# Relative-position tables through DRAM, splits and additions placed elsewhere in an eight-image attention kernel

## The chip, the cores and the metric

The kernel runs on one core of a Trainium2 chip. The core has five engines with a queue each: TensorE (PE, matrix products; its weight loads are listed as PEld), VectorE (DVE), ScalarE (ACT), GpSimd (POOL) and SyncE (SP, which here only issues transfers). An engine works through its queue in order. Products land in PSUM; everything else lies in SBUF or in DRAM. The metric is the device time of one execution in microseconds, as the median of the runs.

## What is computed

Eight images of 32 x 32 positions and 384 channels (1024 tokens each) go through two layers.

```
# layer 0, per image; 6 heads of 64
q, k, v = split(groupnorm(x) @ qkv_w + qkv_b)
s  = (q * 64**-0.5) @ k.T
s += rel_h[:, :, :, :, None] + rel_w[:, :, :, None, :]
#    rel_h[y, x, k] = q[y, x] . rel_pos_h[y - k + 31]
#    rel_w[y, x, k] = q[y, x] . rel_pos_w[x - k + 31]
x  = x + softmax(s) @ v @ proj_w + proj_b
# layer 1
x  = x + causal_attention(layernorm(x))       # one head of 384
x  = x + ffn(layernorm(x))                    # images 0 to 4 only
```

The FFN has sign weights, and after each of its two products it scales by the largest absolute value of the image and clips. So its last step can begin only when the whole image's second product is there.

## The kernel before, in words

One image follows another (`run`, L836). For each there are four stages: `layer0` (L421) with projections, positions and values, then `attend0_fast` (L499), `attention1` (L649), and for images 0 to 4 `ffn` (L766). The path named `g` is entered only if a check of the sums at the end asks for it; in the profile it isn't run.

Products in plain fp32 appear as two records each in the profile. To get nearly fp32 results from the cheaper form fp32r, the kernel splits a value into a high part (rounded to fp32r) and a low part (the remainder) and puts both on different partitions of one tile. For q and k this is `hi_lo` (L428): ACT writes the high part of 64 rows (L429), DVE the low part (L430), from PSUM. Heads go in pairs: `q[par]` and `k[par]` hold, for parity `par`, the high part in one half of the partitions and the low part in the other. `ks` is k with the halves exchanged; POOL copies it (L442, L443). A score tile of 128 keys x 1024 queries is then the sum of three fp32r products (L508): k with q, ks with q, and `unit` with `r`.

`r` carries the relative positions: 32 rows of rel_h and 32 of rel_w for each head, high and low parts. `unit` (L175) spreads them over the 32 x 32 keys. In the kernel before, `positions(g)` (L445) makes them for four image rows and four image columns at a time, for all three pairs at once: 16 fp32 products with a window of 32 table columns as weights and 96 queries (L454), then four casts on ACT (L464) and four subtractions on DVE (L465) of 32 x 384 from PSUM into `r`. Eight groups make an image.

The order in the code is q of the three pairs, k of pair 0, and then eight times a position group and a value product (L470, L385), with k of pairs 1 and 2 between them (`queries_keys`, L434). In `attend0_fast` each pair of heads goes through eight chunks of keys: two score tiles, an exp each on ACT (L512), running sums on DVE (L521), products with v on PE (L526), two chunks behind. At the second chunk of pair 0, `residual` loads x (L105) and POOL adds the bias (L491).

`ffn` ends with a reduction over partitions on POOL (L747), eight clamps on POOL (L833) and eight additions on DVE (L834); then SP stores the image (L856).

The queues are not written out by hand: the framework places each engine's instructions when the kernel is built, by their order in the code and by when their operands are expected, and allots the buffers of a pool as they come free. So products of the next image already run inside the FFN (L375 beside L823), though they come later in the code. The pools that matter are `image` (11 tiles of three rows of 1024), `page` (11 tiles of 128 x 1024), and in PSUM `ps_s` (2 score tiles, also used by the projections) and `ps_o` (4 tiles of 512).

Of the kernel before, what the change touches and what calls it, by code (L numbers as in the profile page):

```python
# [9 lines left out]
F32 = mybir.dt.float32  # L10
# [64 lines left out]
def conv_attn_hybrid(  # L75
# [38 lines left out]
    rel = tile_of("rel", [P, 2, 2 * H - 1])  # L114
    qscale = HD**-0.5

    def load_weights():

        nc.scalar.dma_start(out=bqk, in_=qkv_b[0 : 2 * C].rearrange("(m p) -> p m", p=P))
        for half in range(2):  # L120
            nc.scalar.dma_start(out=rel[half * HD : (half + 1) * HD, 0, :], in_=rel_hT)
            nc.scalar.dma_start(out=rel[half * HD : (half + 1) * HD, 1, :], in_=rel_wT)
# [12 lines left out]
        nc.scalar.mul(rel, rel, 1.0 / qscale)  # L135

# [13 lines left out]
    ones = const.tile([P, P], F32, name="ones")  # L150
# [24 lines left out]
    def make_unit():  # L175

        for i in range(4):
            r = slice(32 * i, 32 * (i + 1))
            nc.gpsimd.tensor_copy(
                unit[r].rearrange("i (h w) -> i h w", h=H), ident[r, r].unsqueeze(2 - i % 2).to_broadcast([32, H, W])  # L180
            )
# [6 lines left out]
    def judge(pools):  # L188

        bad = const.tile([P, 2, N_SEEN], F32, name="bad")  # L190
# [89 lines left out]
    def stages(pools):  # L280
# [140 lines left out]
        def layer0(b, xT):  # L421
# [12 lines left out]
            def queries_keys(m):  # L434
                p = m % NPAIR
                ps = project_T(wqkv_sb, ts(m, P), xT, f"qk_{b}_{m}")
                for par in range(2):
# [3 lines left out]
                    if m >= NPAIR:  # L441
                        nc.gpsimd.tensor_copy(ks[par][hi, p, :], dst[lo].bitcast(F32))  # L442
                        nc.gpsimd.tensor_copy(ks[par][lo, p, :], dst[hi].bitcast(F32))  # L443

            def positions(g):  # L445

                ps = pools.o_tile(f"rel_{b}_{g}")[:, :384].rearrange("p (i n) -> p i n", i=4)
                for i in range(4):
                    at = 4 * g + i
                    win = slice(H - 1 - at, 2 * H - 1 - at)  # L450
                    for par in range(2):
                        qv = q[par].bitcast(F32).rearrange("d p (h w) -> d p h w", h=H)
                        for d in range(2):
                            nc.tensor.matmul(  # L454
                                ps[ts(2 * par + d, 32), i, :], rel[:, d, win], qv[:, :, :, at] if d else qv[:, :, at, :],
                                start=True, stop=True,
                            )
                for d in range(2):
                    for par in range(2):
                        hi, lo = 2 * par + d, 2 * (1 - par) + d  # L460
                        dst = r[par].rearrange("k p (h w) -> k p h w", h=H)
# [443 lines left out]
```

## Time and profile before

| | |
|---|---|
| runs | 2661.9, 2664.29 and 2665.3 us; median 2664.29 |
| profiled execution | 2669.85 us, of which 2667.5 us are the span of the profile |
| granted TensorE clock, mean | 0.993 |
| moved by transfers | 82.00 MB, 31 GB/s over the span |
| image 6, first projection to the first score with all parts | 2104.3 to 2167.6 us |
| image 1, the same, behind an FFN | 404.8 to 462.0 us; part of its projections ran earlier, inside the FFN |

In a line of groups, the fields are the line of code, engine, operation, output and input tiles, shapes and count, then busy us and mean ns of one, then the idle time of the engine just before them and what ended it. In the timeline they are start, duration, engine, line and shape, and in brackets the idle time before. The ends of products are modelled, and neighbours overlap: how far apart two of them start says more than a mean.

### The profile page before, as it was taken

To read this page: it belongs to the slowest core of one execution; us is meant where nothing else is said; L and a number is where in the kernel's file an instruction comes from. 1 tells how busy PE (TensorE), PEld (TensorE's weight loads), DVE (VectorE), ACT (ScalarE), POOL (GpSimd) and SP (SyncE) were. 2 spreads that over 40 slices of the span, in tenths; PEclk is the share of its full clock that TensorE was granted. 3 is DMA by queue.
4 is the path that set the end of the run, shared out by engine and by line. 5 is a ranking of instruction groups with operands and counts; after the bars stand their busy time and mean duration, and the time that the engine had idled before them with its cause. 6 is when DMAs were issued, how large, how long until landed. Compare 5 with 4: busy or idle time off the path is not lost.

```text
span 2667.5 us, 28335 instructions
## 1 busy us (share of the span) xinstructions
PE 2574.1 (96%) x11394; PEld 1540.6 (58%) x11394; DVE 1500.6 (56%) x2373; ACT 1058.2 (40%) x1480; POOL 215.5 (8%) x202
## 2 busy tenths in 40 slices
PE   7989999999999999999999999999999999999998
PEld 4645585555765556755457555576555555455554
DVE  4885466663466644666545656347665356525652
ACT  3431274431555413654127443155541254115421
POOL 2010004000030000030000400003100020002000
PEclk9999999999999999999999999999999999999999
DMA  2501101010010001010110101011000100010000
GB/s 93 202 36 59 36 1 48 1 59 3 33 48 1 29 31 36 1 48 1 60 36 1 48 1 59 1 36 48 1 24 0 48 1 1 24 48 1 1 1 25
DMA packets 34572, 82.00 MB, mean 31 GB/s; under 512 B 5120, under 2 KB 27520, under 8 KB 32896
## 3 DMA queue, kind: packets, MB, share of 16 engines
q1 hardware_dynamic: 28496, 56.43, 6.0%
q0 software_dynamic: 2880, 23.59, 2.6%
q8 instruction: 92, 1.51, 0.2%
q10 hardware_dynamic: 3056, 0.08, 0.1%
q14 instruction: 48, 0.39, 0.0%
HBM read 62.79 MB, written 17.30 MB: 30 GB/s over the span
## 4 chain that ended last, share of the span: by engine, by line
PE 88%; DVE 6%; ACT 3%; issue 1%; POOL 1%; DMA 0%; ACTq 0%; DVEq 0%
PE f_s L508 20%; PE f_av L526 12%; PE f_v L385 8%; PE f_qk L375 8%; PE f_s L680 7%; PE f_av L694 7%; PE f_y L784 6%; PE f_y L823 5%; PE f_q L659 5%; PE f_pj L385 4%; PE f_rel L454 3%; PE f_pt L287 1%; POOL f_y L833 1%; DVE f_r L465 1%; ACT f_h L809 1%
## 5 line engine op out<-in xcount | busy, mean ns | idle before, releaser
L512 ACT ACTIVATE f_pr<-f_s 128x1024 f32<-128x1024 f32 x384 | 393.6, 1026 | 445.5 <-PE f_s L508 431.2
L521 DVE TENSOR_TENSOR f_sum<-f_sum,f_pr 128x1024 f32<-128x1024 f32 x288 | 355.1, 1245 | 228.7 <-ACT f_pr L512 226.7
L526 PE MATMUL f_av<-f_pr,f_v 128*64 128x512 f32 x1536 | 351.8, 598 | 0.0
L375 PE MATMUL f_qk<-f_gnT,wqkv_sb 128*128 128x512 f32 x576 | 265.8, 608 | 5.8 <-DVE f_q L430 4.6
L508 PE MATMUL f_s<-f_q,f_k 128*128 128x512 f32 x768 | 257.8, 415 | 13.4 <-ACT f_pr L512 13.3
L508 PE MATMUL f_s<-f_r,unit 128*128 128x512 f32 x768 | 242.5, 397 | 2.5 <-DVE f_r L465 2.5
L508 PE MATMUL f_s<-f_q,f_ks 128*128 128x512 f32 x768 | 242.1, 396 | 0.0
L526 PEld LDWEIGHTS f_av<-f_pr,f_v 128*64 128x64 f32 x1536 | 101.9, 136 | 199.8 <-issue 192.0
L680 PE MATMUL f_s<-f_q,f_lnT 128*128 128x512 f32 (+3 forms) x576 | 200.1, 491 | 0.0
L694 PE MATMUL f_av<-f_v,f_pr 128*128 128x385 f32 x576 | 194.5, 486 | 0.0
L508 PEld LDWEIGHTS f_s<-f_q,f_k 128*128 128x128 f32 x768 | 125.2, 189 | 119.2 <-issue 48.7
L375 PEld LDWEIGHTS f_qk<-f_gnT,wqkv_sb 128*128 128x128 f32 x576 | 107.4, 193 | 129.2 <-issue 120.6
L465 DVE TENSOR_TENSOR f_r<-f_rel,f_r 32x384 fp32r<-32x384 f32 x256 | 139.7, 553 | 53.3 <-ACT f_r L464 47.2
L508 PEld LDWEIGHTS f_s<-f_r,unit 128*128 128x128 f32 x768 | 143.8, 189 | 40.3 <-DVE f_r L465 6.9
L508 PEld LDWEIGHTS f_s<-f_q,f_ks 128*128 128x128 f32 x768 | 145.2, 189 | 34.9
L694 PEld LDWEIGHTS f_av<-f_v,f_pr 128*128 128x128 f32 x576 | 108.6, 190 | 78.6 <-issue 11.5
L680 PEld LDWEIGHTS f_s<-f_q,f_lnT 128*128 128x128 f32 x576 | 100.7, 190 | 71.5 <-issue 47.4
L464 ACT CAST f_r<-f_rel 32x384 fp32r<-32x384 f32 x256 | 118.8, 469 | 50.8 <-PE f_rel L454 25.7
L385 PE MATMUL f_v<-wqkv_sb,f_gnT 128*128 128x384 f32 x384 | 137.9, 495 | 0.0
L385 PE MATMUL f_pj<-wproj_sb,f_oT 128*128 128x384 f32 x384 | 128.1, 490 | 9.6 <-DVE f_oT L574 9.6
L659 PE MATMUL f_q<-f_lnT,wqk 128*128 128x512 f32 x288 | 129.3, 603 | 0.0
L788 ACT ACTIVATE f_h<-f_y,b_sb 128x256 f32<-128x256 f32 x240 | 100.6, 471 | 67.1 <-PE f_y L784 66.2
(156 smaller groups left out, 3239.3 us busy)
## 6 DMA issues: line engine op xcount, KB each, us to landing
f_gnT<-in_xT SPq DMA_DIRECT2D x24, 512.0 KB, 4.4
f_x<-in_x SPq DMA_DIRECT2D x32, 384.0 KB, 4.3
out_y<-f_x SPq DMA_DIRECT2D x32, 384.0 KB, 2.5
f_w1a<-w1s POOLq DMA_DIRECT2D x5, 1536.0 KB, 6.8
f_w2a<-w2s POOLq DMA_DIRECT2D x5, 1536.0 KB, 7.0
f_wrest<-w1s POOLq DMA_DIRECT2D x5, 768.0 KB, 4.6
f_wrest<-w2s POOLq DMA_DIRECT2D x5, 768.0 KB, 8.6
wqkv_sb<-in_qkv_w SPq DMA_DIRECT2D x3, 576.0 KB, 6.8
```

The source lines that it names most:

```text
L375: nc.tensor.matmul(ps[:, half, :], w[:, k, cols], xT[:, k, ts(half, 512)], start=(k == 0), stop=(k == NC - 1),)
L385: nc.tensor.matmul(ps[:, :C], xT[:, k, ts(j, P)], w[:, k, cols], start=(k == 0), stop=(k == NC - 1))
L465: nc.vector.tensor_tensor(dst[ts(lo, 32)], src, dst[ts(hi, 32)].bitcast(F32), ALU.subtract)
L508: nc.tensor.matmul(sc[:, half, :], keys[:, ts(c, P)], queries[:, ts(half, 512)], start=(i == 0), stop=(i == 2))
L512: nc.scalar.activation(pr, sc.rearrange("p a n -> p (a n)"), AF.Exp)
L521: nc.vector.tensor_tensor(sums[par], prev, prs[par], ALU.add)
L526: nc.tensor.matmul(avs[half][ts(par, HD), :], v[:, c, ts(h, HD)], prs[par][:, ts(half, 512)], start=(c == 0), stop=(c == NJ - 1),)
L659: nc.tensor.matmul(ps, wqk[:, k, ts(m, P)], xT[:, half, k, :], start=(k == 0), stop=(k == NC - 1))
L680: nc.tensor.matmul(sc[:, half, lo:], xT[:, c // 4, k, ts(c % 4, P)], q[:, half, k, lo:], start=(k == 0), stop=(k == NC - 1),)
L694: nc.tensor.matmul(av[:, : C + 1], prs[c][:, ts(j - c, P)], v[:, c, :], start=(c == 0), stop=(c == j))
L784: nc.tensor.matmul(ps, w1k[i // 2][:, ts(m, P)], xs[i % 2][:, half, i // 2, :], start=(i == 0), stop=(i == 2 * NC - 1))
L823: nc.tensor.matmul(ps[:, :C], h, w, start=(i == 0), stop=(i == len(products) - 1))
```

## The change

- **Positions by pair.** `positions(p)` takes one pair at a time. The whole table of both directions (63 columns each, padded to 64, in high and low part: `rel_split`, made once at the start) is multiplied with the pair's q: for each parity and each half of the queries two fp32r products of 128 x 512, summed in PSUM. ACT copies the 64 rows of rel_h from PSUM, DVE those of rel_w with the two image axes exchanged, into a page of 128 x 1024. SP stores both pages to DRAM (`far`) and reads them back with a stride of one row and 32 elements (`near`): so each of the 32 rows gets its window of the table. That is four transfers of 32 x 32 runs of 32 numbers.
- **Splits by pair.** `split(p, near)` writes `r` from `near`: four casts on ACT and four subtractions on DVE of 32 x 1024, from SBUF. Pair 0's stands before the values, pair 1's behind them, and pair 2's inside the attention, behind the first value products of pair 0 (in image 0 before the attention).
- **Order.** All six projections come first, with the position products of pair p behind the next projection, and then the values.
- **Swapped keys.** `ks` is made by four transfers on SP for each pair, instead of POOL.
- **Last additions.** In images 0 to 4 the eight additions and the store of the result are held back until the next image has issued its q, pair 0's keys and its position products. The clamps on POOL stay where they were.
- `unit` is turned round to fit the table's order; the tables are given unreversed. A few constant tiles are smaller or in pages.

```diff
-            def positions(g):
...
+            def positions(p):
+
+                fars = []
+                for par in range(2):
+                    page = pools.page(f"far_{b}_{p}_{par}")
+                    by_col = page.rearrange("i (w h) -> i w h", h=H)
+                    for half in range(2):
+                        ps = pools.o_tile(f"rel_{b}_{p}_{par}_{half}")
+                        for i in range(2):
                             nc.tensor.matmul(
-                                ps[ts(2 * par + d, 32), i, :], rel[:, d, win], qv[:, :, :, at] if d else qv[:, :, at, :],
-                                start=True, stop=True,
+                                ps, rel_split[:, i].rearrange("d a n -> d (a n)"), q[par][:, p, ts(half, 512)],
+                                start=(i == 0), stop=(i == 1),
                             )
+                        nc.scalar.copy(page[:HD, ts(half, 512)], ps[:HD])
+                        nc.vector.tensor_copy(
+                            by_col[HD:, :, ts(half, H // 2)], ps[HD:].rearrange("i (h w) -> i w h", w=W)
+                        )
+                    far = store.tile([P, T], F32, tag=f"far_{p}_{par}", bufs=2, name=f"{pools.path}_far_{b}_{p}_{par}")
+                    nc.sync.dma_start(out=far, in_=page)
+                    fars.append(far)
+                near = pools.page(f"near_{b}_{p}")
+                for par in range(2):
+                    start = fars[par][0:1, 0:1]
+                    for d in range(2):
+                        src = bass.AP(start.tensor, start.offset + d * HD * T, [[T, 32], [T + 32, 32], [1, 32]])
+                        nc.sync.dma_start(
+                            out=near[ts(2 * par + d, 32)].rearrange("m (n o) -> m n o", n=32), in_=src
+                        )
+                return near
+
+            def split(p, near):
                 for d in range(2):
                     for par in range(2):
                         hi, lo = 2 * par + d, 2 * (1 - par) + d
-                        dst = r[par].rearrange("k p (h w) -> k p h w", h=H)
-                        dst = dst[:, :, :, ts(g, 4)] if d else dst[:, :, ts(g, 4), :]
-                        src = ps[ts(hi, 32)].rearrange("k i (p t) -> k p t i" if d else "k i (p t) -> k p i t", p=NPAIR)
+                        dst = r[par][:, p, :].rearrange("k (h w) -> k h w", h=H)
+                        src = near[ts(hi, 32)].rearrange("k (w h) -> k h w" if d else "k (h w) -> k h w", h=H)
                         nc.scalar.copy(dst[ts(hi, 32)], src)
                         nc.vector.tensor_tensor(dst[ts(lo, 32)], src, dst[ts(hi, 32)].bitcast(F32), ALU.subtract)
...
                     if m >= NPAIR:
-                        nc.gpsimd.tensor_copy(ks[par][hi, p, :], dst[lo].bitcast(F32))
-                        nc.gpsimd.tensor_copy(ks[par][lo, p, :], dst[hi].bitcast(F32))
+                        nc.sync.dma_start(out=ks[par][hi, p, :].bitcast(F32), in_=dst[lo].bitcast(F32))
+                        nc.sync.dma_start(out=ks[par][lo, p, :].bitcast(F32), in_=dst[hi].bitcast(F32))
...
-            for m in range(NPAIR):
+            near = []
+            for m in range(2 * NPAIR):
                 queries_keys(m)
-
-            queries_keys(NPAIR)
-            for g in range(NJ):
-                positions(g)
-                if g in (1, 3):
-                    queries_keys(NPAIR + 1 + g // 2)
-                values(g)
+                if 0 < m <= NPAIR:
+                    near.append(positions(m - 1))
+                if m == NPAIR and unfinished:
+                    unfinished.pop()()
+            split(0, near[0])
+            for j in range(NJ):
+                values(j)
+            split(1, near[1])
+
+            later = [lambda: split(2, near[2])]
+            if b == 0 or not pools.fast:
+                later.pop()()
...
                         values(p, pending, sums, avs)
+                        if later:
+                            later.pop()()
...
-                nc.vector.scalar_tensor_tensor(xt[:, j, :], y[:, j, :], s, xt[:, j, :], ALU.mult, ALU.add)
+
+            def add():
+                for j in range(NJ):
+                    nc.vector.scalar_tensor_tensor(xt[:, j, :], y[:, j, :], s, xt[:, j, :], ALU.mult, ALU.add)
+
+            return add
+
+        unfinished = []
...
+                add = ffn(xt, b) if b < B_FFN else None
+
+                def finish(b=b, xt=xt, add=add):
+                    if add:
+                        add()
+                    dst = out[b].rearrange("(j p) c -> p j c", p=P)
+                    for q in range(4):
+                        nc.sync.dma_start(out=dst[:, 2 * q : 2 * q + 2, :], in_=xt[:, 2 * q : 2 * q + 2, :])
+
                 if b < B_FFN:
-                    ffn(xt, b)
-                dst = out[b].rearrange("(j p) c -> p j c", p=P)
-                for q in range(4):
-                    nc.sync.dma_start(out=dst[:, 2 * q : 2 * q + 2, :], in_=xt[:, 2 * q : 2 * q + 2, :])
+                    unfinished.append(finish)
+                else:
+                    finish()
```

## The prediction

> **What bounds the kernel now.** I read the busy times and the chain of waits first, then who TensorE (PE) waits for, then PE's timeline around the change, then the groups by shape, last the DMA issues.
>
> ```profile
> PE 2574.1 (96%) x11394; PEld 1540.6 (58%) x11394; DVE 1500.6 (56%) x2373; ACT 1058.2 (40%) x1480; POOL 215.5 (8%) x202
> ...
> PE 88%; DVE 6%; ACT 3%; issue 1%; POOL 1%; DMA 0%; ACTq 0%; DVEq 0%
> ```
> PE is busy for 96% of the span and is 88% of the chain: PE time taken away is time gained, as long as nothing else comes due first. DVE, ACT and POOL have room on average.
>
> ```profile
> PE f_pt L287 <- DVE xn L364: 17.0, 21, 1.6
> PE f_rel L454 <- ACT f_v L470: 14.4, 5, 3.4
> PE f_s L508 <- ACT f_pr L512: 13.3, 8, 6.0
> ...
> PE f_s L508 <- DVE f_r L465: 2.5, 7, 0.4
> ```
> Columns: total us, times, longest. PE's own idle time is small. The second line occurs five times, once per boundary from an FFN into the next image. In the third, 8.2 us lie in image 0; the other five are 1.02 us each, when the first exp follows a table load behind the last splits.
>
> ```profile
> 413.44 1.52 PE L454 MATMUL f_rel<-f_q,rel 128*32 128x96 f32 x32
> 414.89 2.20 PE L385 MATMUL f_v<-wqkv_sb,f_gnT 128*128 128x384 f32 x6
> ...
> 429.18 1.52 PE L454 MATMUL f_rel<-f_q,rel 128*32 128x96 f32 x32 [3.35 <-ACT f_v L470]
> 430.64 3.61 PE L375 MATMUL f_qk<-f_gnT,wqkv_sb 128*128 128x512 f32 x4
> ```
> One group of positions occupies PE from start to start 1.45 us (1.47 in image 6). At the boundary PE idles 3.35 us, and the next four projection records take 3.61 us where 48 of them take 20.76 us elsewhere (0.4325 each): idling costs twice. The cause is upstream: DVE's queue holds the eight additions (L834), each waiting for a POOL clamp (L833, 414.48 to 422.17 us), so the key split (L430) behind them starts at 423.72 and ACT, which alternates with it, stands for 10.37 us.
>
> ```profile
> L521 DVE TENSOR_TENSOR f_sum<-f_sum,f_pr 128x1024 f32<-128x1024 f32 x288 | 355.1, 1245 | 228.7 <-ACT f_pr L512 226.7
> L465 DVE TENSOR_TENSOR f_r<-f_rel,f_r 32x384 fp32r<-32x384 f32 x256 | 139.7, 553 | 53.3 <-ACT f_r L464 47.2
> L464 ACT CAST f_r<-f_rel 32x384 fp32r<-32x384 f32 x256 | 118.8, 469 | 50.8 <-PE f_rel L454 25.7
> L454 PE MATMUL f_rel<-f_q,rel 128*32 128x96 f32 x2048 | 97.6, 298 | 14.4 <-ACT f_v L470 14.4
> L443 POOL CAST f_ks<-f_k 64x1024 fp32r<-64x1024 f32 x48 | 49.7, 1036 | 329.9 <-ACT f_k L429 327.2
> L660 DVE COPY f_q<-f_q 128x512 f32<-128x512 f32 x32 | 22.1, 691 | 103.8 <-PE f_q L659 103.8
> L660 ACT COPY f_q<-f_q 128x512 f32<-128x512 f32 x16 | 9.4, 585 | 159.3 <-PE f_q L659 159.3
> ```
> These are the prices of what goes and of what comes (mean ns after the busy us).
>
> **What the Trainium skill says.** "FP8 and Floating Point Precision", TensorE Precision Notes: true FP32 makes four passes through the array; the reduced form, a truncation, is listed apart. The trace agrees: a 512-column fp32 projection costs 2 x 0.4325 us, while FFN products on fp32r operands (L784, own weight load each) follow every 0.231 us (six in 1.386). "TensorE: Matmul & The Clock Gate", Part 1: after about 3.4 us idle the array runs at half clock; the 3.61 us above fits. "DMA: Bandwidth & Descriptors", Anatomy of one DMA: about 2 us fixed each; the 384 KB stores land in 2.5 us. "SBUF — State Buffer", Who interferes with whom: a DVE instruction with two SBUF inputs and a POOL instruction reading SBUF exclude each other. The trace agrees: three sums of 1.245 us take 9.95 us from 136.21, while POOL's 6.74 us addition (L491) runs.
>
> **The change, part by part.**
>
> *Position products.* 64 groups x 1.46 us = 93.4 us of PE go. 8 images x 3 pairs x 8 = 192 products of 128x512 on fp32r operands with an own weight load come: 192 x 0.231 = 44.4 us. All of it is on the path: **-49.0 us**. Least certain is the form; attention already multiplies the same fp32r q at 24 in 5.77 us, so I take it.
>
> *Evacuations and splits.* Per image DVE loses 32 x 0.553 = 17.7 us and gets 12 copies of 64x512 from PSUM (0.691) and 12 subtractions of 32x1024 (priced as L521, 1.245) = 23.2 us; ACT loses 15.0 and gets 12 x 0.585 + 12 x 1.03 (L512's 1024 elements) = 19.4. In the 63 us before attention of image 6 DVE is busy 36.3 us and ACT 31.3; with two of three splits there they stay near 37 and 31 of about 57. PE's cover is two score and four output PSUM tiles, two projections (10.4 us) or four value products (8 us): at those shares the work hides, cost 0; uncovered it would be 5 us an image.
>
> *The way through DRAM.* Per pair two stores of 512 KB, then four gathers of 1024 runs of 128 B, each waiting on SP for the stores. The store lies between 2.5 us (384 KB) and 3.8 us (768 KB): 3 us, both 4. The gather has no row of its own. The nearest is the bias load of 1536 four-byte runs (6.0 KB), which lands in 4.2 us:
>
> ```profile
> out_y<-f_x SPq DMA_DIRECT2D x32, 384.0 KB, 2.5
> ...
> b_sb<-in_b ACTq DMA_DIRECT2D x1, 6.0 KB, 4.2
> ```
> That bounds a run at (4.2 - 2) x 16 / 1536 = 23 ns on each of 16 engines; the queue's own share (3.1% of 16 engines in 60 us, 3056 packets) gives 10 ns. With 6 ns for the bytes (POOL's queue: 2.6% of 16 x 2667.5 us over 2880 packets of 8 KB is 385 ns): 16 to 29 ns; the upper end would be the mean packet of the main queue, 90 ns (6.0% of 16 x 2667.5 us over 28496, about 2 KB each). I take 25: 4096 runs are 256 an engine, 6.4 us, landing 8.4 us after the issue. From the first projection: pair 0's products end at 12.3 us, evacuated 14.5, stored 19, gathered 27; pairs 1 and 2 follow 7 us apart, 34 and 41. Six projections and three position blocks end at 37, values at 54. So split 0 is due 10 us after its data and pair 2's is needed 75 us later still. Cost 0, between 0 and rival B's price.
>
> *Swapped keys.* POOL loses 12 copies of 1.036 us, off the path. SP gets 12 transfers of 256 KB per image, about 0.5 us to issue and 3 us to land, used 25 us later at the earliest. On SP they queue among stores and gathers, some 30 issues (15 us) in 57; behind them wait only the output stores and the next x, needed after attention. Cost 0, 3 us an image if keys of pair 0 came last.
>
> *Additions moved.* They no longer stand before the keys. The clamps still end about 17 us after the FFN. PE by then has finished the third q, the products and pair 0's keys, so some additions go on waiting on DVE, but with projections left for PE. Gone are at most 14.4 us idle and 5.5 us of half-clock records (3.61, 3.67, 1.98, 1.98, 2.88 against 1.73); I take **-16**. Their output stores move behind pair 0's key transfers, whose readers come 30 us later: 0.
>
> *The end of the stage.* The last splits leave the path: of 5 x 1.38 us (0.36 + 1.02) and 2 x 0.36, 7.6 us, I take **-5**; the table load stays.
>
> *Split 2 inside attention* (seven images). It puts 4.1 us on ACT and 5 on DVE among exps. ACT's gap while PE does values and the next score is about 3.6 + 1.4 - 1.2 = 3.8 us, so exps slip by up to 0.7 us: **+5**. Between 0 (spread out, or done earlier) and 4.1 x 7 = 29.
>
> *Port.* Subtractions now read two SBUF operands, where before one was PSUM; one meeting the 6.7 us POOL addition stands still. Values' tiles cover most: **+2**, bounds 0 and 5 x 4.
>
> The first image gains as the others: its binarization waits for the last value product; the three new set-up instructions on the table are under 1 us and lie beside the weight loads. Sum: -49 - 16 - 5 + 5 + 2 = -63. The profiled execution took 2669.85 us (span 2667.5 and 2.3 around it): 2606.9. It is 5.6 us above the median of the runs, 2664.29, so the forecast for a median is **2601**; its own range 2588 (all 27.5 us of stalls gone, nothing new) to 2615.
>
> **Rivals.** (A) *Splits queued ahead of their data.* If the planner puts them into ACT's and DVE's queues some 6 us before the gather lands, key evacuations stand behind them; PE's two score tiles cover part, 4 us an image remain (3 to 5): 2601 + 32 = 2633. For it: ACT and DVE have early gaps to be filled. Against: 10 us of slack.
>
> (C) *The additions are planned as early as before.* DVE then stands until 422 us, position copies and keys wait, PE runs dry for about 6 us per boundary: 30 us instead of the 19.9 of now, so 26 worse than forecast: 2627. For it: other work is plainly reordered (projections run inside the FFN). Against: lower priority than the evacuations.
>
> (B) *Slower: the gather's run costs 90 ns.* Then a pair needs 23 us on the DMA engines, pairs follow one another, landing at 44, 67 and 90 us. Split 1 stands in ACT's queue ahead of the first exp, due at 53: 14 us lost per image, 112 in all; with -49 - 21 the net is +42, **2706**. It decides above 53 + 70/8 = 62 us for pair 1, about 75 ns a run. For it: no gather of 128 B is in the trace. Against: the bias load's 23 ns.
>
> (D) *The products don't run as single reduced ones.* As fp32, 24 x 0.865 = 20.8 us an image instead of 11.7: +73 instead of -49, 2723.
>
> **Chances.** Main case 0.56, A 0.15, C 0.14, B 0.11, D 0.02, something that cancels within 0.2% (5.3 us, about what a measurement can tell) 0.02. Faster 0.85, same 0.02, slower 0.13. The range takes the main case, C and A to their far end: 2588 to 2641.
>
> **What would show it.** Right: position products at 0.23 us and 45 us in all; no line of values waiting at FFN boundaries; gathers landing within 10 us; the stage before attention near 56 us in image 6. Wrong: ACT or DVE idle on a gather before a split (A, B); DVE idle on POOL clamps with keys behind them (C); position products in pairs of records (D).

## The result and the profile after

The median is **2663.65 us** (2659.76 to 2665.27, four runs) against 2664.8 for the kernel before (2661.9 to 2665.69, four runs): a ratio of **0.9995 [0.9978, 1.0013]**. No change can be measured where 2601 was forecast and 2588 to 2641 given as the range. The profiled execution took 2665.27 us (span 2663.5).

Below, a difference between two kernels in us is the difference of their ratios to the kernel before, times 2665. By the intervals such a difference is good to some 5 to 9 us.

First the page of the kernel after: the engines' busy times, and the shares of the chain.

```profile
PE 2547.0 (96%) x9538; PEld 1526.1 (57%) x9538; DVE 1603.2 (60%) x2311; ACT 1130.0 (42%) x1417; POOL 112.0 (4%) x106
...
PE 27%; DVE 1%; ACT 1%; issue 0%; DVEq 0%; ACTq 0%
```

PE lost 1856 products but only 27 us of busy time; DVE and ACT, which were to gain 44 and 35 us (8 images at 23.2 − 17.7 and 19.4 − 15.0 us), gained 103 and 72. The granted clock fell from 0.993 to 0.982, so what remains of PE's work runs slower. The chain is followed through only 29% of this span, so the waits are read instead. PE's, in the kernel after (total us, times, longest):

```profile
PE f_qk L381 <- DVE f_k L436: 31.4, 8, 3.9
PE f_pt L293 <- DVE xn L370: 16.5, 18, 1.9
...
PE f_s L541 <- ACT f_pr L545: 10.6, 13, 1.4
...
PE f_v L391 <- ACT f_v L497: 3.0, 8, 0.4
```

The old line of 14.4 us at the FFN boundaries is gone. In its place stands a new first line, of a kind that the kernel before did not have: a projection that waits for the split of a key, once in every image, 3.9 us each. PE's timeline at the boundary that the prediction showed (image 1; start, us, work, idle before):

```profile
414.09 2.43 PE L464 MATMUL f_rel<-f_q,rel_split 128*128 128x512 f32 x8
416.35 5.31 PE L381 MATMUL f_qk<-f_gnT,wqkv_sb 128*128 128x512 f32 x12
421.10 2.42 PE L464 MATMUL f_rel<-f_q,rel_split 128*128 128x512 f32 x8
423.35 5.31 PE L381 MATMUL f_qk<-f_gnT,wqkv_sb 128*128 128x512 f32 x12
432.59 7.81 PE L381 MATMUL f_qk<-f_gnT,wqkv_sb 128*128 128x512 f32 x11 [3.92 <-DVE f_k L436]
```

The position products are as cheap as forecast: from 416.35 to 423.35 are 7.00 us, 12 projection records at 0.4325 take 5.19 of them, and 1.81 are left for 8 products, 0.226 each. The loss stands in the last line. The sixth projection idles 3.92 us, and its 11 records then take 7.81 us where 12 took 5.31.

ACT, over the same time:

```profile
421.70 1.11 ACT L435 ACTIVATE f_k<-f_qk,bqk 64x1024 fp32r<-64x1024 f32 x1 [2.86 <-PE f_qk L381]
428.70 2.24 ACT L435 ACTIVATE f_k<-f_qk,bqk 64x1024 fp32r<-64x1024 f32 x2 [5.89 <-PE f_qk L381]
431.16 1.11 ACT L435 ACTIVATE f_k<-f_qk,bqk 64x1024 fp32r<-64x1024 f32 x1 [0.21 <-DVE f_k L436]
432.29 2.03 ACT L468 COPY f_far<-f_rel 64x512 f32<-64x512 f32 x4
```

One key evacuation, then 5.89 us of standing for a projection, then three more. The order of instructions in ACT's queue says why. This is its listing for image 0 as the kernel is built (row, line, output <- input; projections 3, 4 and 5 are the keys of pairs 0, 1 and 2). The trace, which leaves the numbers of the tiles out, has the same order of lines in every image:

```
29 L435 f_k_0 <- f_qk_3
30 L435 f_k_0 <- f_qk_4
31 L435 f_k_1 <- f_qk_3
32 L435 f_k_1 <- f_qk_4
33 to 36 L468 f_far_2 <- f_rel_2 (four copies, position products of pair 2)
37 L435 f_k_0 <- f_qk_5
38 L435 f_k_1 <- f_qk_5
```

Row 30 is queued **ahead of row 31**. It needs projection 4, which PE finishes 5.3 us later; row 31, whose data lie ready, reads the second half of score tile 3. There are two score tiles, so projection 5 needs tile 3 back. PE finishes projection 4 and then stands until row 31 and its DVE half are done. Everything behind it on ACT, the copies of pair 2's positions too, comes later as well.

Next the costliest groups that answer to those shown of before, then the DMA issues of the kernel after.

```profile
L554 DVE TENSOR_TENSOR f_sum<-f_sum,f_pr 128x1024 f32<-128x1024 f32 x288 | 343.7, 1222 | 161.6 <-ACT f_pr L545 160.2
L492 DVE TENSOR_TENSOR f_r<-f_near,f_r 32x1024 fp32r<-32x1024 f32 x96 | 187.6, 1954 | 25.6 <-ACT f_r L491 23.0
L491 ACT CAST f_r<-f_near 32x1024 fp32r<-32x1024 f32 x96 | 146.0, 1521 | 2.3
L469 DVE COPY f_far<-f_rel 64x512 f32<-64x512 f32 x96 | 62.7, 692 | 1.6
L464 PE MATMUL f_rel<-f_q,rel_split 128*128 128x512 f32 x192 | 56.2, 435 | 0.0
L468 ACT COPY f_far<-f_rel 64x512 f32<-64x512 f32 x96 | 48.4, 581 | 33.8 <-PE f_rel L464 33.6
```

```profile
f_far<-f_far SPq DMA_DIRECT2D x48, 512.0 KB, 3.0
f_ks<-f_k SPq DMA_DIRECT2D x96, 256.0 KB, 5.1
...
f_near<-f_far SPq DMA_DIRECT2D x96, 128.0 KB, 3.9
out_y<-f_x SPq DMA_DIRECT2D x32, 384.0 KB, 3.9
```

The copies cost what was taken (0.692 and 0.581), the gathers of 1024 runs land in 3.9 us and not in 8.4, but a cast costs 1.52 us on average, not 1.03, and a subtraction 1.95, not 1.245.

### The profile page after: what moved, and what is told of

The parts are those of the page before. It is cut to its first block, busy times and chain, and to the rows that moved or that the text cites. A ratio compares the mean times of both kernels' runs of the same rounds, so it can differ in the third digit from the quotient of the medians.

```text
span 2663.5 us, 24967 instructions
## 1 busy us (share of the span) xinstructions
PE 2547.0 (96%) x9538; PEld 1526.1 (57%) x9538; DVE 1603.2 (60%) x2311; ACT 1130.0 (42%) x1417; POOL 112.0 (4%) x106
## 5 line engine op out<-in xcount | busy, mean ns | idle before, releaser
L554 DVE TENSOR_TENSOR f_sum<-f_sum,f_pr 128x1024 f32<-128x1024 f32 x288 | 343.7, 1222 | 161.6 <-ACT f_pr L545 160.2
L559 PE MATMUL f_av<-f_pr,f_v 128*64 128x512 f32 x1536 | 359.3, 599 | 0.0
L381 PE MATMUL f_qk<-f_gnT,wqkv_sb 128*128 128x512 f32 x576 | 280.7, 638 | 37.2 <-DVE f_k L436 31.4
L541 PE MATMUL f_s<-f_q,f_k 128*128 128x512 f32 x768 | 260.8, 419 | 10.6 <-ACT f_pr L545 10.6
L381 PEld LDWEIGHTS f_qk<-f_gnT,wqkv_sb 128*128 128x128 f32 x576 | 115.7, 205 | 171.2 <-issue 161.9
L492 DVE TENSOR_TENSOR f_r<-f_near,f_r 32x1024 fp32r<-32x1024 f32 x96 | 187.6, 1954 | 25.6 <-ACT f_r L491 23.0
L729 PEld LDWEIGHTS f_av<-f_v,f_pr 128*128 128x128 f32 x576 | 108.8, 190 | 78.4 <-issue 11.5
L491 ACT CAST f_r<-f_near 32x1024 fp32r<-32x1024 f32 x96 | 146.0, 1521 | 2.3
L391 PE MATMUL f_v<-wqkv_sb,f_gnT 128*128 128x384 f32 x384 | 127.3, 489 | 3.0 <-ACT f_v L497 3.0
L723 ACT ACTIVATE f_pr<-f_s 128x1024 f32<-128x1024 f32 (+3 forms) x64 | 41.6, 650 | 208.7 <-DVE f_s L720 208.7
```

Of the source, the lines that this page charges most:

```text
L381: nc.tensor.matmul(ps[:, half, :], w[:, k, cols], xT[:, k, ts(half, 512)], start=(k == 0), stop=(k == NC - 1),)
L391: nc.tensor.matmul(ps[:, :C], xT[:, k, ts(j, P)], w[:, k, cols], start=(k == 0), stop=(k == NC - 1))
L491: nc.scalar.copy(dst[ts(hi, 32)], src)
L492: nc.vector.tensor_tensor(dst[ts(lo, 32)], src, dst[ts(hi, 32)].bitcast(F32), ALU.subtract)
L541: nc.tensor.matmul(sc[:, half, :], keys[:, ts(c, P)], queries[:, ts(half, 512)], start=(i == 0), stop=(i == 2))
L554: nc.vector.tensor_tensor(sums[par], prev, prs[par], ALU.add)
```

## The experiments

### The order of the keys

Theory: the time went into the queue's order, which the swapped keys' transfers brought with them (Q in the texts below; in the later ones S says that the way of swapping the keys has no price of its own, and its rival K that it has). Rivals: ACT and DVE have too much work before the attention (W), or transfers are in the way (T). The first kernel puts the keys of pairs 1 and 2 behind all that comes before them in the code. In each image two entries move on ACT (projection 4's, rows 30 and 32 of the listing, now behind the four copies) and two on DVE; nothing else moves on these two, and the queues of PE, SP and POOL stay as they are.

```diff
-                    hi_lo(dst, hi, lo, ps, bqk[:, m : m + 1])
+                    made = hi_lo(dst, hi, lo, ps, bqk[:, m : m + 1])   # now returns both
+                    if m > NPAIR:
+                        for i in made:
+                            tc.keep_in_program_order(i)
```

> The changed kernel with one thing different: on ScalarE and VectorE the evacuations of k of pairs 1 and 2 are queued behind everything that the code lists before them, so that both parities of pair 0's k leave PSUM before pair 1's. Same instructions, same transfers; only eight entries move in each image. Theory Q (queue order: ScalarE stands for projection 4 while half of projection 3's score tile is unread, projection 5 needs that tile, TensorE idles 3.92 us and then works at half clock for some 3 us): the 3.92 us wait is gone in all eight images and so are the slow records behind it: 8 x 7 = 56 us, about 2610 us, ratio to before near 0.98. Rival W (evacuations and splits are too much work for the two engines in this stage, and the wait only shows there first): the wait comes back at the values or at the first scores, at most 15 us gained, 2650 us or more. Rival T (the 63 MB of added transfers slow the memories for everyone): no change, 2660 us.

Measured: 2619.55 us, 0.9838 [0.9814, 0.9862], **42 us below the change as made** with the same work; the theory had named up to 56. Its waits on key splits and on exps, and its PE timeline at the same boundary:

```profile
PE f_s L541 <- ACT f_pr L545: 10.4, 13, 1.4
...
PE f_qk L381 <- DVE f_k L437: 6.0, 5, 2.3
```

```profile
416.46 5.31 PE L381 MATMUL f_qk<-f_gnT,wqkv_sb 128*128 128x512 f32 x12
422.34 5.39 PE L381 MATMUL f_qk<-f_gnT,wqkv_sb 128*128 128x512 f32 x12 [0.56 <-DVE f_k L437]
```

Eight waits of 3.92 us are gone, five shorter ones are left at the FFN boundaries, and with the idle time the slow records go. What the clock took, (1 − granted clock) times the length, summed over all stretches of 5 us, is 20.6 us before, 48.6 after and 21.0 here. The theory holds for these 42 us; a mere lack of room on ACT and DVE, or transfers in the way, would have left the time where it was.

Is it the transfers that brought the order? The next kernel is the change with `ks` copied by POOL again, with nothing pinned.

```diff
-                        nc.sync.dma_start(out=ks[par][hi, p, :].bitcast(F32), in_=dst[lo].bitcast(F32))
-                        nc.sync.dma_start(out=ks[par][lo, p, :].bitcast(F32), in_=dst[hi].bitcast(F32))
+                        nc.gpsimd.tensor_copy(ks[par][hi, p, :], dst[lo].bitcast(F32))
+                        nc.gpsimd.tensor_copy(ks[par][lo, p, :], dst[hi].bitcast(F32))
```

> The changed kernel with the swapped keys made by four GpSimd copies for each pair again, as before the change, instead of transfers. Theory Q: without the transfers the planner puts both parities of pair 0's k ahead of pair 1's on ScalarE and VectorE, so the 3.92 us wait is gone as in the kernel with the order mended, and the time is within 10 us of it, about 2610 us. Rival W: 2650 us or more. Rival T: only the 25 MB of these transfers go of 63, so at most a third of what they cost comes back, 2640 us or more, and the wait for k stays.

Measured: 2645.45 us, 0.993 [0.9912, 0.9948], 17 us below the change, where Q had put some 2610. Both halves of projection 3 now lead ACT's queue without help. But another wait came; its two lines:

```profile
PE f_v L391 <- DVE f_far L469: 21.1, 7, 4.1
...
PE f_qk L381 <- DVE f_k L436: 11.5, 5, 2.4
```

So the wait on key splits falls from 31.4 to 11.5 us, while pair 2's table copies now stand behind keys, and values wait for their PSUM tiles. The order of the keys does hang on who makes `ks`, but the whole order changes with it, so this kernel prices nothing alone.

Five more kernels with POOL's copies or with more pinned were to price the transfers alone.

```diff
+                        if p < 2:                          # splits 0 and 1: in code order
+                            for i in made:
+                                tc.keep_in_program_order(i)
...
+            values(1)                                     # values in a written order, pinned
             split(0, near[0])
+            for j in (0, 2, 3, 4, 5, 6, 7):
+                if j == 6:
+                    split(1, near[1])
                 values(j)
```

The first has POOL's copies, and keys 1 and 2 and splits 0 and 1 in code order (the first part of the diff); the second has the values written out as well (pinned from the third on).

> GpSimd makes the swapped keys again, and on ScalarE and VectorE the k evacuations of pairs 1 and 2 and the splits of pairs 0 and 1 keep the order of the code. Theory Q: when both ways of swapping keys have their evacuations in order, they take the same time, within 8 us of the 2619.6 us of the kernel with transfers in order; the 21 us of waiting of the values for table copies, which the kernel with GpSimd's copies still had, are gone, so they were an order of the queue too. Rival K (the way of swapping has its own price: 12 GpSimd copies of 1.04 us an image that shut VectorE out, or 25 MB of transfers): a difference of 20 us or more, 2640 us as measured with the planner's own order, or 2600 us.

> GpSimd makes the swapped keys again, and ScalarE's and VectorE's queues are pinned to nearly the order that the kernel with transfers and keys in order has: k as in the code, split 0, values' copies, split 1 ahead of the last values' copies (the run before had put split 1 behind all of them, and its six us of casts then stood ahead of the first exp). Theory S: the way of swapping has no price of its own, only the order that the planner makes of it: 2612 to 2628 us. Rival K: GpSimd's copies cost 20 us or more by themselves: 2640 us or more.

Measured: 2692.67 us, 1.0098 [1.0063, 1.0134], and 2670.27 us, 1.0012 [1.0001, 1.0023]. Neither is what it was meant to be. In the first, split 1 now stands behind all copies of values and ahead of the first exp, and PE waits 52.7 us for exps (7.9 at most), which neither S nor K had foreseen. In the second, copies of values stand ahead of the last keys, and PE waits 4.1 us for the first exps in images 1 to 5. Both are confounded; what they show is the spread that order can make.

Pinned twins followed: all but the first value's copy held, once with POOL's copies and once with transfers, and, since the free copy then stood ahead of the last keys on DVE with POOL's copies, a third with that one pinned too.

> Swapped keys by GpSimd's copies, with k of pairs 1 and 2, splits 0 and 1 and values' copies all pinned to the order of the code (values 1 first, split 1 ahead of values 6 and 7), the same for its twin with transfers. Theory S (the way of swapping has no price of its own): within 8 us of the twin, both 2612 to 2632 us. Rival K (GpSimd's copies cost 20 us or more themselves): 20 us or more above the twin.

> The twin: swapped keys by transfers, pinned to the same order. Theory S: within 8 us of the kernel with GpSimd's copies, 2612 to 2632 us. Rival K: 20 us or more below it.

> Swapped keys by GpSimd's copies, with every values' copy pinned too, so that ScalarE and VectorE have the queue of the kernel with transfers and pinned order (2623 us). Theory S (no price of its own: the 30 us between the pair were the one entry): 2615 to 2631 us. Rival K (GpSimd's copies lengthen what VectorE does beside them: the last additions took 1.23 us on average instead of 0.81, and a copy queued behind the clamps comes late): 10 to 25 us above the twin, 2633 to 2648 us.

Measured: POOL 2653.15 us, 0.9947 [0.993, 0.9965]; transfers 2623.29 us, 0.9825 [0.98, 0.985]; POOL with the free copy held 2636.79 us, 0.9889 [0.9868, 0.991]. The last two are the nearest pair, and **between them the transfers are 17 us ahead** (0.9889 − 0.9825, so 17 with an uncertainty of some 9). They are near, not equal. ACT's queue is the same in images 0 to 5; DVE's differs by one addition at each FFN boundary, and in image 0 by where the work on the sign weights stands; and PE takes the first scores earlier among the values where POOL copies. With POOL's copies the eight additions on DVE take 0.979 us each instead of 0.805, and PE's wait for exps is 18.0 us instead of 10.4. Attention in images 1 to 5 takes 116.7 us instead of 114.7; image 0's goes the other way, 131.9 instead of 142.3. So the change's own idea for `ks` was rather a gain than a loss; the order that came with it cost 42 us.

### The splits

All further kernels stand on the first one (keys in order). Theory: half of the casts and subtractions are dear because they step through `near` by 32 numbers, 128 bytes. Rival: all are dearer by something else, such as POOL or the transfers. This kernel reads `near` straight for both halves, with every queue in the same order, PE's and the transfers' too. It leaves out the exchange of the image axes in the rel_w rows.

```diff
-                        src = near[ts(hi, 32)].rearrange("k (w h) -> k h w" if d else "k (h w) -> k h w", h=H)
+                        src = near[ts(hi, 32)].rearrange("k (h w) -> k h w", h=H)
```

> The kernel with the keys in order, but the splits of the rel_w rows read their page straight through, without exchanging the two image axes: the rows come out permuted, all else is the same, every queue in the same order. A cast then takes some 1.04 us instead of 2.0 and a subtraction 1.21 instead of 2.0: 3 us less on each of the two engines for a pair, 9 us an image. Theory H (the forecast's: PSUM tiles hide the splits, cost 0): no change, 2620 us. Rival W (in the images behind an FFN, and where split 2 meets the first exps, the two engines set the time): the 10 us of waits for exps, 6 us for k and 3 us for values shrink, 8 to 15 us gained, 2605 to 2612 us.

Measured: **2604.13 us**, 0.9777 [0.976, 0.9793], 16 us below the kernel that it stands on. The casts and subtractions there (keys in order), then here (shortest/median/longest ns of one):

```profile
L491 ACT CAST f_r<-f_near x96: 1040/1506/2122, 59.4 to 2401.2; 32x1024 fp32r<-32x1024 f32 x96
L492 DVE TENSOR_TENSOR f_r<-f_near,f_r x96: 1211/1920/8080, 61.4 to 2408.8; 32x1024 fp32r<-32x1024 f32 x96
```

```profile
L491 ACT CAST f_r<-f_near x96: 1040/1043/1051, 59.0 to 2375.4; 32x1024 fp32r<-32x1024 f32 x96
L492 DVE TENSOR_TENSOR f_r<-f_near,f_r x96: 1211/1218/6640, 60.9 to 2382.5; 32x1024 fp32r<-32x1024 f32 x96
```

A straight cast takes 1.04 us and a straight subtraction 1.21; with the step they take about 2.0. The Trainium skill names a likely mechanism: "SBUF — State Buffer", Specifications (TRN2), says that SBUF has lines of 16 bytes and that full bandwidth needs at least two hits in each. A step of 128 bytes has one. The page gives no price; here it is a factor of 1.7 to 2. The trace agrees that the step costs; no run varies the step, so that the lines are the reason is not shown. The wait for exps (10.4 us) leaves the list of large ones, and attention of images 1 to 5 falls from 114.7 to 112.8 us.

Can the step be put on the write instead?

```diff
-                        dst = r[par][:, p, :].rearrange("k (h w) -> k h w", h=H)
-                        src = near[ts(hi, 32)].rearrange("k (w h) -> k h w" if d else "k (h w) -> k h w", h=H)
+                        dst = r[par][:, p, :].rearrange("k (h w) -> k w h" if d else "k (h w) -> k h w", h=H)
+                        src = near[ts(hi, 32)].rearrange("k (a n) -> k a n", n=32)
```

> The kernel with the keys in order, with the exchange of the two image axes moved from the reading to the writing side of the split of the rel_w rows: a cast reads its page straight through and writes r with a stride; a subtraction reads one operand straight, the other with the stride, and writes with it. Theory W (the strided reading cost 2.0 us where 1.04 and 1.21 were priced, and those microseconds show as waits for exps, keys and values: 15 us when all of it was left out): casts fall to 1.04 us, subtractions stay between 1.2 and 2.0, and half or all of the 15 us come back, 2604 to 2612 us. Rival (writing with the stride is as slow as reading with it): 2620 us.

Measured: 2618.13 us, 0.9816 [0.9803, 0.9829]; means of 1.526 and 2.016 us. For the cast, which here reads straight and writes with the step, a strided write is as dear as a strided read; the subtraction has the step in one input and in the write.

Split 2 before the attention in all images, instead of inside it:

```diff
-            if b == 0 or not pools.fast:
-                later.pop()()
+            later.pop()()
```

> The kernel with the keys in order, with split 2 issued before the attention in all images. Theory P (the forecast's prices): the stage's end gets its 5 us of waiting back and the exps lose the 5 us that split 2 costs among them: no change within 5 us, 2620 us. Rival V (a split ahead of the first exp stands there in full: 6.1 us of casts at the measured 1.04 and 2.0 us, less 2 us of cover, in seven images, with slow records behind): 30 us or more lost, 2650 us, as split 1 behind the values did.

Measured: 2615.93 us, 0.9807 [0.9791, 0.9823]; the intervals overlap with those of the kernel that it stands on. Only five pairs of neighbours change places on ACT, and none on DVE: the planner sets these casts among the first exps wherever the code has them. Whether split 2 would be dearer truly ahead of the attention was not tried.

### The additions

The additions of the FFN's end, at once as before; then, in a second kernel, pinned behind what the code has ahead of them.

```diff
-                if b < B_FFN:
-                    unfinished.append(finish)
-                else:
-                    finish()
+                finish()
```

> The kernel with the keys in order, but the last additions and the store of an FFN image are issued at its end, as before the change. Theory: holding the additions back is worth what the forecast named less what still waits: the waits for k at the FFN boundaries (6.0 us idle in the kernel with keys in order, some 4 us slow) stand where 14.4 us idle and 5.5 us slow stood, so 10 us come back, about 2630 us. Rival C of the prediction: without the move the wide table copies and keys queue behind all eight additions and TensorE runs dry for 6 us and more at each of five boundaries, 20 us more than with it, 2640 us. Rival N: the planner places the additions by itself where they lie now; no difference, 2620 us.

> The kernel with the keys in order, and the eight additions pinned on VectorE behind both halves of pair 0's k and pair 2's table copies, as the code lists them; the planner had put four of them ahead of each half. Theory: the waits for k at the FFN boundaries (6.0 us idle, two of them long enough for slow records behind them, some 2 us each) go: 9 us less, about 2610 us. Rival: the additions then stand before the k of pair 1 on VectorE, and what waited for pair 0's k waits for that or for the values' copies; no difference, 2620 us.

Measured: 2656.97 us, 0.9965 [0.995, 0.9979], 34 us above its base and more than theory (10) or rival C (20) had named, and 2621.85 us, 0.9834 [0.9813, 0.9856], no difference. The first has the line of the prediction's rival C:

```profile
PE f_rel L464 <- DVE f_q L437: 30.8, 5, 6.3
```

DVE stands on the clamps with q's split behind the additions, about 6 us in each of five boundaries, as C had priced it. In the second the waits for keys go, and the waits for copies of values grow from 3.1 to 12.4 us (8, 2.3 at most): at these boundaries, it seems, DVE and ACT have as much as fits, and what stands first decides only where PE waits.

### Products and transfers, doubled

```diff
-                        for i in range(2):
+                        for i in (0, 1, 0, 1):
```

> The kernel with the keys in order, and each pair of position products issued twice into the same PSUM tile (the second time from the start again, so the values are the same): 192 more products of 128x512. Theory: position products lie on the path and cost 0.231 us each, so 44 us more, about 2664 us. Rival (they lie in time in which TensorE would wait for evacuations anyway): 15 us more or less, 2635 us at most.

Measured: 2665.69 us, 0.9996 [0.9984, 1.0007]: 192 more products cost 42 us, 0.22 each. Some of that is order: the planner also placed table copies and splits otherwise on ACT and DVE. By stages, the 24 products of an image add 5.1 us ahead of the attention in images 6 and 7, where 5.3 are due, and 3.0 in images 1 to 5, and the attention is 0.9 to 2.2 us longer though it holds none of them.

Then both the gathers and the key transfers doubled; and the gathers alone, the second of each going into DRAM that nobody reads.

```diff
-                    for d in range(2):
+                    for d in (0, 1, 0, 1):
...
-                    if m >= NPAIR:
+                    for _ in range(2 * (m >= NPAIR)):
```

```diff
+                        spare = store.tile([32, T], F32, ...)
+                        nc.sync.dma_start(out=spare.rearrange("m (n o) -> m n o", n=32), in_=src)
```

> The kernel with the keys in order, with every gather from the tables and every transfer of swapped keys issued twice: 38 MB and 24 issues more in each of eight images together. Theory (transfers cost nothing on the path): within 6 us of 2620 us, gathers landing later but before their splits. Rival B in small (the queue on SP and the DMA engines already decide when the splits can run): the second copies push the splits behind the first exps, 4 us or more an image, 2650 us or more.

> The kernel with the keys in order, with each gather from the tables followed by a second one of the same runs into DRAM that nobody reads: 96 transfers and 12.6 MB of 128-byte runs more, and no instruction that waits for them but SP's. Theory (the transfers' own cost is nothing; in the kernel with everything twice the time went to another place of split 2 and to the loads of the first image): within 8 us of 2620 us. Rival T (the gathers' 1024 runs each delay the keys' transfers, x, and the splits): 15 us or more, 2635 us or more.

Measured: 2673.49 us, 1.0031 [1.0019, 1.0044], 51 us above the base; and 2638.24 us, 0.9893 [0.9878, 0.9908], 15 us above. The first is confounded: the planner also moved split 2's casts among the exps, attention of images 1 to 5 went from 114.7 to 122.2 us, and image 0's from 135.6 to 153.9, where PE stands 8.6 us for the load of `wkT`. The second meets its rival T, not the theory. It isn't clean either, since ACT's and DVE's queues differ from the base in over 25 places each. Its attention is 12.8 us longer in image 0 and 3.3 in images 1 to 5, where the stage before it is 1.4 us shorter; in images 6 and 7 both stages stay within 0.2 us. So doubled gathers are not free, most is paid in image 0, and how much of it is order stays open. In image 0 weights are loaded through the same queue. That suggested the last kernel, with the loads of `wqT` and `wkT` on POOL's queue:

```diff
-        nc.sync.dma_start(out=wqT_sb, in_=wqT.rearrange("(k p) c -> p k c", p=P))
-        nc.sync.dma_start(out=wkT_sb, in_=wkT.rearrange("(k p) c -> p k c", p=P))
+        nc.gpsimd.dma_start(out=wqT_sb, in_=wqT.rearrange("(k p) c -> p k c", p=P))
+        nc.gpsimd.dma_start(out=wkT_sb, in_=wkT.rearrange("(k p) c -> p k c", p=P))
```

> The kernel with the keys in order, with the two tables of weights that image 0 multiplies out once (they need no slot but a free one, and before the change were loaded at 12 us) issued from GpSimd's queue instead of SP's, where they had come to stand behind the new transfers until 67 us. Theory S0 (SP's queue delays them, their product, the room for the sign weights' loads, and so the sign weights and image 0's attention, by 11 us): the product lies near 80 us instead of 93, image 0's attention is 10 us shorter, about 2608 us in all. Rival (image 0's attention is bound by VectorE's work on the sign weights whatever their loads do): no change, 2619 us.

Measured: 2624.26 us, 0.9838 [0.9819, 0.9856], no gain. The product of these weights came at 76.1 us instead of 93.1, but DVE's sums of the sign weights began later than before (103.6 instead of 95.7), behind running sums, and image 0's attention took 133.9 us, with 82.6 instead of 74.6 ahead of it. Late loads of these two weights are not what makes image 0's attention longer.

## Why the prediction was wrong

By stages, from the traces (us; "up to the attention" is from the first score of layer 1 of the image before, in image 0 from the start, to the first score product with `r`; attention is from there to the first product of the last division, L601 in the kernel after):

| | before | after | keys in order | and splits straight |
|---|---|---|---|---|
| image 0 up to the attention | 88.1 | 80.8 | 74.6 | 73.6 |
| images 1 to 5, mean | 187.9 | 183.2 | 178.4 | 176.6 |
| images 6 and 7, mean | 110.7 | 108.9 | 102.6 | 101.9 |
| attention, image 0 | 124.8 | 136.1 | 135.6 | 132.8 |
| attention, images 1 to 5 | 112.4 | 114.7 | 114.7 | 112.8 |
| attention, images 6 and 7 | 111.6 | 112.8 | 112.8 | 112.8 |

The gain was there and was given back in the same stage (5 to 6 us an image) and in the attention.

**The step that failed** is "Evacuations and splits", with its cost of 0: "PE's cover is two score and four output PSUM tiles … at those shares the work hides". Average shares cannot say this. Two score tiles cover a delay only if the evacuations come in the order in which the tiles are wanted back. The prediction let "Swapped keys" cost 0 on SP and asked who is queued behind the transfers; it did not ask what the planner would do with the instructions that feed them. That is 31.4 us of idle time and the slow records behind it, **42 us** by experiment, two thirds of the miss of 62.6. Rivals A and C were about order too, but named other instructions: ACT waits only 2.3 us ahead of all casts, so A did not come; C's additions do stand ahead of pair 0's keys on DVE in the kernel after (421.13 and 425.43 us), but the wait is set by ACT.

**The term that was mis-sized** is the same step's cast and subtraction: 1.03 and 1.245 us hold for the straight half (1.04 and 1.21), while the other half takes 2.0. The diff showed the exchange of axes in `src`; I priced only the element count. **16 us** by experiment. With both mended the time is 2604, beside the forecast of 2601; that it comes so near is in part luck, since other terms below were off both ways, and that kernel leaves out the exchange.

Point by point:

- *Position products*, −49: right (0.226 us each; doubled, +42 for a forecast of 44.4, some of it order). Rival D fell.
- *The way through DRAM*, 0: right for the change as made, where no wait of PE or ACT names a gather, with a price of a run that was too high (landing in 3.9 us, not 8.4). The 2 us that it took off as fixed are stated in the section that it names for transfers issued by POOL; these are issued by SP. Rival B fell.
- *Additions moved*, −16: right in kind. The line of 14.4 us is gone, and undoing the move costs 34 us where the sum with C's price was 26 above the forecast. With the keys in order 6.0 us of waits remain at these boundaries.
- *End of the stage*, −5: not seen. The wait for exps went from 13.3 to 10.6 us only; with straight splits it leaves the list, so this too is the strided half.
- *Split 2 inside attention*, +5 in all: attention is 2.3 us longer in each of images 1 to 5, of which the straight splits take back 1.9, and 1.2 in images 6 and 7, which they do not. No kernel had split 2 out of the attention, so its share of the rest is not shown.
- *Port*, +2: no wait of PE shows it; single subtractions reach 7.8 us beside POOL's addition. Not separated.
- *"The first image gains as the others"*: wrong. Its stage before gains 7.3 us, but its attention is 11.3 us longer. 6.0 of both are one thing: the 18 products for `wqk` (L277 before, L283 after) ran ahead of the attention, at 81.6 us, and now stand inside it, at 99.3. Both stages together take 212.9 us before, 216.9 after, 210.2 with the keys in order and 206.4 with straight splits as well. The other 5 us are idle time. Before, PE waits 8.3 us for exps in this attention; after, 2.7 us for exps and once 10.8 us for a copy on ACT, which itself stands for a transfer. The two lines, PE's and ACT's:

```profile
PE f_den L589 <- ACT f_oT L578: 10.8, 1, 10.8
```

```profile
ACT f_oT L578 <- DMA w2s<-f_sign: 12.3, 1, 12.3
```

The transfer is the last store of sign weights, issued at 153.7 us, before at 136.3. In all 17 changed kernels the copy begins within 0.3 us after that store has landed; before, 4.7 us after it and without a wait for it. Both tiles come from the pool `image`, so the copy probably takes the tile that the store frees; that is inferred. With POOL's copies of `ks` and nothing pinned, the store is issued at 141.1 us, PE has no such wait, and image 0's attention is 129.4 us.

**What stays open.** Why the sign weights are stored 17 us later than before: with the product of `wqk` early again (76.1 us) their last store still came at 158.5. And why the planner puts pair 1's first half ahead of pair 0's second when `ks` goes by transfers; the runs show that it does, not why.

The best versions with all of the computation are the one with keys in order and its near twins, 2616 to 2624 us, whose intervals overlap: some 1.7% below both kernels.

## What to carry to other kernels

Where a planner orders the queues, an edit is priced on the whole order. Here two instructions an image, on each of two queues, stood in front of their neighbours, which cost 42 us, and who copied one tile decided whether they did; kernels with the same computation lay between 2616 and 2693 us. For work that hides behind a small pool of buffers, ask in which order the buffers come back, not how busy the engines are. And price an operation by its access pattern as well as by its element count: an exchange of axes on SBUF data in a diff is a candidate for a factor of two (the copy out of PSUM with exchanged axes, 0.692 us, paid nothing).

## What was not expected of the hardware

- With a step of 128 bytes in SBUF a cast of 32x1024 takes ACT about 2.0 us instead of 1.04, whether it reads or writes with the step, and a subtraction takes DVE about 2.0 instead of 1.21; DVE's copy out of PSUM with exchanged axes (64x512) takes 0.692 us, like a straight one before (0.691 for 128x512).
- In the kernel with keys in order an idle time of 0.56 us leaves the next 12 projection records at 5.39 us, but 2.07 us of it (image 2) leaves them at 7.08. The Trainium skill's "TensorE: Matmul & The Clock Gate", Part 1, speaks of an idle window of about 3.4 us; here less than that was followed by slow records.
- A gather of 1024 runs of 128 bytes (128 KB) lands in 3.4 to 3.9 us (medians of the kernels); in the kernel after it is 3.9, as for a plain store of 384 KB there.
- In the five kernels with POOL's copies of 1.04 us, DVE's additions of 128x384 take 0.98 to 1.23 us on average, in those with transfers 0.61 to 0.89; in the nearest pair 0.979 and 0.805.
